# Re-cutting the side streams of a scan stage and issuing attention in written order, in a Mamba, expert, attention and FFN block on one core

## The chip, the cores and the metric

The kernel runs on one core of a Trainium2 chip. The metric is the device time in microseconds from the kernel's start to its end; times are given as the median of several runs. A profiled execution is a further run with the hardware profiler on; its span is the time from its first to its last instruction.

## The reference, cut to what matters

The input x has 4 sequences of 512 tokens and 128 channels. Four residual layers follow one another: a Mamba block with a mixture of experts behind it, an FFN, a latent attention, and the same FFN again.

```python
x = x + attn_a(layernorm(x))   # Mamba, then 8 experts, top 2
x = x + ffn(layernorm(x))      # 128 -> 384 -> 128, silu(gate) * up
x = x + attn_b(layernorm(x))   # 16 heads of 8, causal, low-rank q and k
x = x + ffn(layernorm(x))
# in attn_a, for every token t, 256 channels and 16 states:
dA = exp(delta[t] * A);  h = dA * h + (delta[t] * u[t]) * B[t];  y[t] = sum_n(h * C[t])
# then the experts:
out = out + w_e * (silu(hs @ Wg[e]) * (hs @ Wu[e])) @ Wd[e]
```

The recurrence in `h` is what makes the scans: for each of 4 sequences and 16 states one scan along 512 tokens, for 256 channels.

## The kernel before

**Tiles.** A sequence is 4 tiles of 128 tokens (NT = 4); 256 channels are 2 halves of 128 partitions (NE = 2). The program has two stages. In the first, 64 scans (4 sequences x 16 states) run one after another. In the second, attention runs over 16 groups G of 4 heads; two groups make a unit u (8 heads of one sequence), 8 units in all.

**A scan step** (`scan`, L844). For state n of sequence b: ACT makes the decay `da` (L796) two steps ahead and SP loads `cs` (L800); PE spreads a row of B over the partitions, `pb` (L806); DVE multiplies it with `du` to `bx` (L838) and scans `hst` (L858); POOL multiplies with C to `hc` (L870); PE adds `hc` over the states into `yp` with four matmuls (L816). `bx` and `pb` have one buffer each, `hst` two.

**Side streams.** All else in the first stage is written as Python generators and put beside the scans: `ahead` (the `front` of the next sequence: norm, convolution, projections, softplus), `closing` (`close`, `route`, `number`, `scatter`: gate, output projection, routing, and writing the tokens to DRAM by expert), `tokens` (`combine`, the first FFN, `project` to q and k), `tiles` (`experts`, one tile of 128 rows per step) and `rest` (`early`: statistics of the later sequences, zeros, weights). A stream's step has two halves: `begin` runs to the generator's next yield and is traced between the scan and the product `hc`; `end` runs to the yield after it and is traced behind the product `bx` of the next scan (`halves`, L569). A half that yields "sc" wants the two shared PSUM tiles of that tag; in a scan only the first stream that wants them gets its `end`, the others wait for the next scan with theirs. `hc` waits for the DVE instructions that the `begin` halves issued (L876).

**Who orders the work.** Inside `tc.manual_schedule(engines=ORDERED)` the instructions of PE, DVE, ACT and SP are issued in the order in which the code writes them. The scans and three turns after them are in such a block (L978, L1013). The second stage, from L1219 on, is not: there a planner of the language orders each engine's instructions by its own priorities.

**Experts.** Groups of sequences are [0], [1] and [2, 3], with 15, 15 and 23 tiles of rows. `experts` plans which rows belong to which expert (DVE, L272 to 299), then takes a tile per step: SP stores the tile of three steps ago, loads rows and weights (L341 to 357), PE transposes (`mpt`), forms gate and up (`mpg`, `mpu`, L370) and down (`mpd`, L382), ACT does tanh (`thm`), DVE the two products (L320, L321) at the next `begin`. `combine` gathers each token's two rows back with POOL's indirect DMAs (`yk`, L403) and adds them one turn later (L395).

**Attention.** `project` (L496) makes q and k, splits them into three bf16 parts on POOL and stores them (`q_d`, `k_d`); `fill(u)` (L1063) loads a unit's `qs` and `ks` with six DMAs on SP. `maxima(u)` (L1074) forms scores on PE and their row maxima on DVE (L1084), 22 tiles a unit, and writes the maxima into `qs` through DRAM. `exps(G)` (L1124) forms the scores again with the maxima taken off and exponentiates on ACT (`p`, L1154), ten steps a group. `weigh(G)` (L1157) multiplies by the values (f32, `po`, L1166). In the loop over G (L1230) each of ten steps takes a score, one or two maxima and a piece of the weigh of the group before; side streams get `rate` turns a step. Sequences' last FFNs (`last`) start at units 3, 5 and 7, that of sequence 3 stands alone at the end.

The roots of the layer norms are made on DVE by an integer guess and three Newton steps (`rsqrt`, L131).

Of the kernel before, what the change touches and what calls it, by code (L numbers as in the profile page):

```python
# [8 lines left out]
F32 = mybir.dt.float32  # L9
# [28 lines left out]
def block_kernel(ctx, tc, x, rms1_w, rms2_w, in_proj_w, conv_w, conv_b, x_proj_w,  # L38
# [172 lines left out]
    def number(b):  # L211

        hit = hits[b]
        both = tmp("both", [NT, NEXP], BF16)
        nc.vector.tensor_tensor(both, hit[:, :, 0], hit[:, :, 1], ALU.add)
        yield
        pr = ps.tile([P, 2, NT, NEXP], F32, tag="mm", name="prank")
        for i, m in enumerate((before, ones)):
            nc.tensor.matmul(
                pr[:, i].rearrange("p j e -> p (j e)"), m, both.rearrange("p j e -> p (j e)"),  # L220
                start=True, stop=True,
            )

        tot = tmp("ctot", [NEXP, NT])
        nc.scalar.copy(tot, pr[:, 1].rearrange("p j e -> p e j"))
        ahead = tmp("cahead", [NT, NEXP])
        nc.scalar.copy(ahead, pr[:, 0])
        yield
        inc = tmp("cinc", [NEXP, NT])
        nc.vector.tensor_tensor_scan(  # L230
            inc.rearrange("p e j -> p (e j)"), restart.rearrange("p e j -> p (e j)"),
            tot.rearrange("p e j -> p (e j)"), 0.0, ALU.mult, ALU.add,
        )
        g, at = place[b]
        free = regions[ROWS[g]] if at == 0 else taken[g]
        taken[g] = end = tmp("cend", [NEXP])
        nc.vector.tensor_tensor(end, free, inc[:, :, NT - 1], ALU.add)
        nc.vector.tensor_tensor(inc, inc, tot, ALU.subtract)
        nc.vector.tensor_tensor(
            inc, inc, free.unsqueeze(2).to_broadcast([P, NEXP, NT]), ALU.add  # L240
        )
        row = tmp("crow", [NT, NEXP])
        nc.vector.tensor_tensor(row, inc.rearrange("p e j -> p j e"), ahead, ALU.add)
        rows2 = tmp("crows", [NT, 2, NEXP])
        nc.vector.tensor_tensor(
            rows2, hit, row.unsqueeze(2).to_broadcast([P, NT, 2, NEXP]), ALU.mult
        )
        rowf = tmp("crowf", [NT, 2])
        nc.vector.tensor_reduce(rowf, rows2, AX.X, ALU.add)
        nc.vector.tensor_copy(rows[b], rowf)  # L250
        yield

    def scatter(b):
# [3 lines left out]
        for t in range(NT):  # L257
            for k in range(2):
# [6 lines left out]
                if (2 * t + k) % 3 == 2:  # L265
                    yield
                    yield
# [55 lines left out]
    def experts(g):  # L323
# [8 lines left out]
        n = NTILES[g]  # L332
        xt, xT, wgu, wd, hidden, ys, of = {}, {}, {}, {}, {}, {}, {}
        for i in range(-1, n + 3):
            if i - 2 in hidden:
# [53 lines left out]
    def combine(b):  # L389
# [3 lines left out]
        for t in range(NT + 1):  # L393
            for k, yk in enumerate(got):
                nc.vector.scalar_tensor_tensor(  # L395
                    base[b][:, t - 1, :], yk, gates[b][:, t - 1, k : k + 1],
                    base[b][:, t - 1, :], ALU.mult, ALU.add,
                )
            yield
            new = []  # L400
            for k in range(2 if t < NT else 0):
                yk = wt.tile([P, C], F32, tag="yk", name="yk", bufs=4)
# [5 lines left out]
            got = new  # L408
# [184 lines left out]
    with ExitStack() as first:  # L593
# [42 lines left out]
        for k in ("r0", "m0", "r01", "m01"):  # L636
            norms[k] = w1.tile([P, B * NT], F32, tag=k, name=k)

        def deviations(seqs):
            n = len(seqs) * NT  # L640
            cols = slice(seqs[0] * NT, seqs[0] * NT + n)
            r0, m0, r01, m01 = (norms[k][:, cols] for k in ("r0", "m0", "r01", "m01"))
            v = w1.tile([P, n], F32, tag=f"v{n}", name="v0")
            mean, var = (mv0.rearrange("p b t s -> p (b t) s")[:, cols, k] for k in range(2))
            nc.vector.tensor_scalar(v, var, EPS, None, ALU.add)
            rsqrt(v, n, w1, "ln", r0)
            less(mean, r0, n, to=m0)
            nc.vector.tensor_tensor(v, r0, r0, ALU.mult)
            nc.vector.tensor_tensor(v, v, var, ALU.mult)
            nc.vector.tensor_scalar(v, v, EPS, None, ALU.add)  # L650
            rsqrt(v, n, w1, "rms", r01)
            nc.vector.tensor_tensor(r01, r01, r0, ALU.mult)
            less(mean, r01, n, to=m01)

        def early():

            for b in range(1, B):
# [3 lines left out]
            deviations(range(1, B))  # L661
# [39 lines left out]
        def front(b):  # L701

            h0[b] = h = w2.tile([P, NT, C], F32, tag="h0", name=f"h0_{b}")
            hn = w1.tile([P, NT, C], F32, tag="hn", name="hn")
            cols = slice(b * NT, (b + 1) * NT)
            scaled(hn, xs[b], norms["r01"][:, cols], norms["m01"][:, cols])
            scaled(h, xs[b], norms["r0"][:, cols], norms["m0"][:, cols])
# [6 lines left out]
            for e in range(NE):  # L714
                yield "sc"
                pm = ps_s.tile([P, L], F32, tag="sc", name="pm")
                for k in range(KW):
                    nc.tensor.matmul(
# [3 lines left out]
                pms.append(pm)  # L722
                if e == NE - 1:
                    for i in range(NE):
                        nc.scalar.activation(xi[b][:, i, :], pms[i], AF.Silu, bias=cb[:, i, :])
                yield
            yield
# [6 lines left out]
            yield  # L734
            yield "sc"
# [7 lines left out]
            nc.scalar.copy(dt[b], pm[0:DTR, :])  # L743
            pm = ps_s.tile([P, L], F32, tag="sc", name="pbc")
# [9 lines left out]
            cr = w1.tile([2 * NS, L], F32, tag="bc_c", name="bc_c")  # L754
            nc.scalar.copy(bc[b], pm[0:96, :])
            nc.scalar.copy(cr, pm[0 : 2 * NS, :])
            c_d[b] = dram1.tile([NS, L], F32, tag="c_d", name="c_d")
            nc.sync.dma_start(c_d[b], cr[NS:, :])
            yield
            nc.vector.tensor_tensor(rest, pm[0:96, :], bc[b], ALU.subtract)  # L760
            nc.scalar.copy(mid, rest)
            yield "sc"
            nc.gpsimd.tensor_copy(bc[b][32:64, :], mid[32:64, :])
            nc.gpsimd.tensor_tensor(bc[b][64:96, :], rest[64:96, :], mid[64:96, :], ALU.subtract)
# [4 lines left out]
            du[b] = r = w2.tile([P, NE, L], F32, tag="du", name=f"du_{b}")  # L769
            for e in range(NE):  # L770
# [5 lines left out]
                nc.scalar.activation(r[:, e, :], pd, AF.Relu, bias=dtb[:, e, :])  # L776
            nc.scalar.activation(y, y, AF.Exp, scale=-1.0)
            nc.scalar.activation(dl, y, AF.Ln, bias=1.0)
            nc.scalar.activation(d, y, AF.Identity, bias=1.0)
            yield  # L780
            nc.vector.scalar_tensor_tensor(d, d, -1.0, y, ALU.add, ALU.subtract)
            yield
            yield
# [100 lines left out]
        def close(b):  # L884
# [12 lines left out]
            for t in range(NT):  # L897
                for e in range(NE):
# [3 lines left out]
                    )  # L902
            h2 = wt.tile([P, NT, C], F32, tag="h2", name="h2", bufs=1)
            nc.scalar.copy(h2, po)
            yield
            yield
            nc.gpsimd.tensor_tensor(h2, h0[b], h2, ALU.add)
            yield
# [20 lines left out]
            yield  # L929
# [6 lines left out]
            nc.scalar.copy(lg, pl)  # L936
            yield
# [40 lines left out]
        with tc.manual_schedule(engines=ORDERED):  # L978
# [5 lines left out]
            next(first)  # L984

# [18 lines left out]
            for b in range(B):  # L1004
                if b:
                    closing.add(close(b - 1), start(b - 1), scatter(b - 1))
                for n in range(NS):
                    if n == 4 and b + 1 < B:
# [11 lines left out]
    with ExitStack() as second:  # L1020
# [200 lines left out]
        while 0 not in stores:  # L1221
            turn(*streams)
        fill(0)
        fill(1)
        for _ in times(2, maxima(0)):
            turn(*streams)
        begin = {3: (0,), 5: (1,), 7: (2,)}
        rate = {0: 1.2, 1: 1.0, 2: 0.8, 3: 0.8, 4: 0.8, 5: 0.8}
        filled, credit = 2, 0.0
        for G in range(2 * UNITS + 1):  # L1230
            u = G // 2
            if G % 2 == 0:
                ends.add(*(last(b) for b in begin.get(u, ())))
                while filled < min(u + 3, UNITS) and filled // 2 in stores:
                    fill(filled)
                    filled += 1
                if u < UNITS and u % 2 == 0:
                    values(u // 2)
                while u + 1 < UNITS and filled <= u + 1:
                    turn(*streams)  # L1240
                    if filled // 2 in stores:
                        fill(filled)
                        filled += 1
                more = maxima(u + 1) if u + 1 < UNITS else iter(())
            scores = exps(G) if G < 2 * UNITS else iter(())
            weighed = weigh(G - 1) if 1 <= G else iter(())
            for step in range(10):
                credit += rate.get(u, 0.4)
                while credit >= 1.0:
                    turn(*streams)  # L1250
                    credit -= 1.0
                next(scores, None)
                next(weighed, None)
                for _ in range(1 + step % 2):
                    next(more, None)
            run(weighed)
            if G % 2 == 1:
                run(more)
        while any(stream.gens for stream in streams):
            turn(*streams)  # L1260
        run(last(B - 1))
# [56 lines left out]
```

## Time and profile before

| | us |
|---|---|
| Median of 3 runs | 958.27 |
| Lowest, highest | 956.39, 960.52 |
| Profiled execution | 962.98 |
| Its span | 960.9 |
| First scan starts, last scan starts | 49.3, 428.2 |
| First scores with exponentials | 547.1 |
| PE, DVE, ACT, POOL busy | 757.7, 565.0, 413.4, 316.0 |
| Mean granted TensorE clock | 0.852 of full |

Of the page, a group's line gives the engine, the operation, what it writes and reads, its count, its busy time in us and the mean of one in ns, and after the second bar how long the engine was idle just before these instructions and for whom it waited. Here are some of the rows that the work below uses:

```profile
L870 POOL TENSOR_TENSOR hc<-hst,cs 128x1024 f32<-128x1024 f32 x64 | 150.5, 2355 | 161.8 <-DVE mh L321 39.3
L858 DVE TENSOR_TENSOR_SCAN hst<-da,bx 128x1024 f32<-128x1024 f32 x64 | 146.3, 2286 | 6.9
L838 DVE TENSOR_TENSOR bx<-du,pb 128x1024 f32<-128x1024 f32 x64 | 78.3, 1223 | 16.4 <-PE pb L806 12.1
L1166 PE MATMUL po<-p,va 128*32 128x512 f32 (+3 forms) x512 | 73.2, 451 | 0.0
```

In lines of the timeline the first number is the start in us from the span's start, the second how long it took; what stands in brackets is the idle time before it and who ended it.

### The profile page before, as it was taken

The numbers are of one execution on the slowest core, as the hardware profiler recorded it, in microseconds if no ns is written. First come the engines' busy times: TensorE is split into PE (matmuls) and PEld (weight loads), VectorE is DVE, ScalarE is ACT, GpSimd is POOL, SyncE is SP. The second block draws the span as 40 slices with busy tenths as digits, with TensorE's granted clock in tenths as the row PEclk, the third lists the DMA queues.
The fourth block names the chain that finished last, engine by engine and source line by source line (L and its number), as shares of the span: only waits on it lengthen the run. The fifth ranks groups of instructions, "written<-read, shape, count | busy, mean of one in ns | idle before, by whom it ended". The sixth has DMA issues, their size and how long they took to land. (4 is left out here: it accounts for less than half of the span.)

```text
span 960.9 us, 11946 instructions
## 1 busy us (share of the span) xinstructions
PE 757.7 (79%) x3763; PEld 425.7 (44%) x3763; DVE 565.0 (59%) x1154; ACT 413.4 (43%) x798; POOL 316.0 (33%) x247
## 2 busy tenths in 40 slices
PE   4449777859897867887685899999569999999964
PEld 1114233227644624555553676873233435454432
DVE  3197687878777886883375543434750543666411
ACT  2635726824666432423301344443025435645641
POOL 1135474574427564563205103001404031000010
PEclk9768879959998987898857899998575959999997
DMA  3018321128424515433753546773102303120000
GB/s 101 34 33 338 126 65 56 47 81 251 149 72 139 167 56 156 123 117 121 191 128 107 173 141 221 242 197 74 33 2 80 85 19 92 37 47 3 3 12 11
DMA packets 84479, 99.16 MB, mean 103 GB/s; under 512 B 10369, under 2 KB 56457, under 8 KB 83241
## 3 DMA queue, kind: packets, MB, share of 16 engines
q1 hardware_dynamic: 78881, 87.09, 30.6%
q0 software_dynamic: 4352, 10.89, 3.7%
q8 instruction: 30, 0.49, 0.2%
q10 hardware_dynamic: 1184, 0.43, 0.2%
q14 instruction: 32, 0.26, 0.1%
HBM read 76.67 MB, written 21.63 MB: 102 GB/s over the span
## 5 line engine op out<-in xcount | busy, mean ns | idle before, releaser
L870 POOL TENSOR_TENSOR hc<-hst,cs 128x1024 f32<-128x1024 f32 x64 | 150.5, 2355 | 161.8 <-DVE mh L321 39.3
L816 PE MATMUL yp<-hc,ident 128*128 128x512 f32 x256 | 152.3, 724 | 31.3 <-POOL hc L870 29.6
L858 DVE TENSOR_TENSOR_SCAN hst<-da,bx 128x1024 f32<-128x1024 f32 x64 | 146.3, 2286 | 6.9
L1084 DVE TENSOR_REDUCE mx<-sc 128x1 f32<-128x384 f32 (+3 forms) x168 | 103.3, 635 | 69.5 <-PE sc L1092 67.8
L1154 ACT ACTIVATE p<-st 128x512 f32<-128x512 f32 x160 | 90.7, 598 | 52.6 <-PE st L1149 50.1
L816 PEld LDWEIGHTS yp<-hc,ident 128*128 128x128 f32 x256 | 53.2, 221 | 126.2 <-POOL hc L870 83.3
L1088 PE MATMUL sc<-ks,qs 72*128 72x128 bf16 (+3 forms) x256 | 78.1, 367 | 34.0 <-issue 14.2
L796 ACT ACTIVATE da<-delta,A 128x512 f32<-128x512 f32 (+1 forms) x128 | 84.5, 713 | 29.4 <-DVE hst L858 26.7
L838 DVE TENSOR_TENSOR bx<-du,pb 128x1024 f32<-128x1024 f32 x64 | 78.3, 1223 | 16.4 <-PE pb L806 12.1
L320 DVE SCALAR_TENSOR_TENSOR thm<-thm,mpg 128x512 f32<-128x512 f32 x53 | 36.1, 681 | 81.6 <-ACT thm L376 81.6
L370 PE MATMUL mpg<-xTm,wgu 128*128 128x128 f32 x424 | 67.5, 304 | 9.3 <-DVE thm L320 4.3
L1166 PE MATMUL po<-p,va 128*32 128x512 f32 (+3 forms) x512 | 73.2, 451 | 0.0
L370 PEld LDWEIGHTS mpg<-xTm,wgu 128*128 128x128 f32 x424 | 60.7, 216 | 21.4 <-issue 6.8
L1141 PE MATMUL st<-qs,ks 75*128 75x512 bf16 (+3 forms) x256 | 63.5, 317 | 1.7 <-DMA qs<-m_d 0.8
L382 PE MATMUL mpd<-wd,mh 128*128 128x128 f32 x424 | 58.8, 280 | 5.5 <-ACT xTm L363 5.3
L370 PE MATMUL mpu<-xTm,wgu 128*128 128x128 f32 x424 | 61.6, 291 | 1.1 <-DMA wgu<-in_Wu_dram 1.1
L806 PE MATMUL pb<-bc,pick 96*128 96x512 bf16 x64 | 27.5, 430 | 41.9 <-DVE bx L838 40.4
L370 PEld LDWEIGHTS mpu<-xTm,wgu 128*128 128x128 f32 x424 | 57.3, 208 | 1.6 <-issue 0.6
L382 PEld LDWEIGHTS mpd<-wd,mh 128*128 128x128 f32 x424 | 52.9, 195 | 9.4 <-ACT xTm L363 7.7
L363 ACT ACTIVATE xTm<-mpt,r2w 128x128 f32<-128x128 f32 x53 | 19.4, 367 | 87.5 <-PE mpt L361 64.6
L1092 PE MATMUL sc<-maskq,identb 128*128 128x128 bf16 (+2 forms) x176 | 51.8, 294 | 0.0
L259 POOL DMA_INDIRECT xg<-hs,rows x32 | 34.3, 1071 | 52.6 <-DVE cends L280 44.3
(244 smaller groups left out, 1111.3 us busy)
## 6 DMA issues: line engine op xcount, KB each, us to landing
cs<-c_d SPq DMA_DIRECT2D x64, 256.0 KB
wgu<-in_Wg_dram SPq DMA_DIRECT2D x53, 256.0 KB
wgu<-in_Wu_dram SPq DMA_DIRECT2D x53, 256.0 KB
wd<-in_Wd_dram SPq DMA_DIRECT2D x53, 256.0 KB
xg<-zero SPq DMA_DIRECT2D x8, 1024.0 KB
k_d<-parts POOLq DMA_DIRECT2D x12, 384.0 KB
qs<-q_d SPq DMA_DIRECT2D x24, 192.0 KB
ks<-k_d SPq DMA_DIRECT2D x24, 192.0 KB
```

Of the source, the lines that this page charges most:

```text
L370: nc.tensor.matmul(pp[:, f, :], w[:, k, f * P : (f + 1) * P], rows_in, start=True, stop=True,)
L382: nc.tensor.matmul(pd, hT[:, f, :], w[:, f, :], start=(f == 0), stop=(f == NFC - 1))
L796: nc.scalar.activation(da[:, e, e:], delta[b][:, e, e:], AF.Exp, scale=A[:, e, n : n + 1])
L816: nc.tensor.matmul(yps[b][:, e, :], ident, hc[:, e, :], start=(n == 0), stop=(n == NS - 1))
L838: nc.vector.tensor_tensor(bxs[s], du[s // NS], taps[s][1].unsqueeze(1).to_broadcast([P, NE, L]), ALU.mult)
L858: nc.vector.tensor_tensor_scan(hst.rearrange("p e l -> p (e l)"), dec.pop(s).rearrange("p e l -> p (e l)"), bxs.pop(s).rearrange("p e l -> ...
L870: done = nc.gpsimd.tensor_tensor(hc, hst, cs.unsqueeze(1).to_broadcast([P, NE, L]), ALU.mult).ins
L1084: nc.vector.tensor_reduce(*taken, AX.X, ALU.max)
L1088: nc.tensor.matmul(sc[:, c : c + w], q[0:NP9, h, t * P : w], k[0:NP9, h, 0:w], start=(h == h0), stop=False, skip_group_check=True,)
L1141: nc.tensor.matmul(pt[:, c : c + L - kt * P], k[0 : NP9 + 3, h0 + j, rows], q[0 : NP9 + 3, h0 + j, kt * P : L], start=(c == 0), stop=False ...
L1154: nc.scalar.activation(p, pt, AF.Exp, scale=scale)
L1166: nc.tensor.matmul(po[32 * j : 32 * j + 32, kt * P : L], vs[b % 2][:, kt, c : c + 32], got[j][kt], start=(kt == 0), stop=(kt == NT - 1),)
```

## The change

It has four parts.

1. **Norms of the first layer.** `deviations` makes both inverse roots (of the layer norm, and of layer norm and RMS norm together) in one `rsqrt` of double width; sequence 1's statistics move from the first scans into the prologue. `front` writes its scaled input into the tile "xn" of another pool and makes `h0` behind `sz`.
2. **Side streams in the scans.** `front` starts at a sequence's first scan instead of its fifth; the convolution's eight matmuls come in four steps instead of two; pdt, pbc and pd, and Exp, Ln and the DVE products of softplus, get steps of their own. `close` adds `h0` on DVE straight from PSUM, and has fewer empty halves; `number` ends without a yield; `scatter` issues two DMAs per step instead of three. `experts` has an empty step before its first tile step and one after it.
3. **combine** adds a gathered row two turns after its gather instead of one, with six buffers instead of four.
4. **Attention.** The whole second stage's loop stands in `tc.manual_schedule(engines=ORDERED)`. A turn's `begin` halves stand ahead of a step's score, maxima and weigh, its `end` halves behind them; the weigh comes behind the maxima. Two more turns run between the first fills and the first maxima. `rate` is 0.7 for units 0 to 4 and 0.5 beyond, instead of 1.2 falling to 0.8, then 0.4, and a step has one turn at most.

The diff, cut to its core:

```diff
 def number(b):
         nc.vector.tensor_copy(rows[b], rowf)
-        yield
 def scatter(b):
-                if (2 * t + k) % 3 == 2:
+                if k and t < NT - 1:
                     yield
                     yield
 def experts(g):
         n = NTILES[g]
+        yield
+        yield
         for i in range(-1, n + 3):
+            if i == 0:
+                yield
+                yield
 def combine(b):
-        for t in range(NT + 1):
-            for k, yk in enumerate(got):
+        for t in range(NT + 2):
+            for k, yk in enumerate(got.pop(0) if t > 1 else ()):
...
-            got = new
+            got.append(new)
 def deviations(seqs):
+            nc.vector.tensor_scalar(v[:, 0], var, EPS, None, ALU.add)
+            nc.vector.tensor_scalar(v[:, 1], var, 1.0 + EPS, EPS * EPS, ALU.mult, ALU.add)
+            rsqrt(v.rearrange("p k b t -> p (k b t)"), 2 * n * NT, w1, f"ln{n}",
+                  r.rearrange("p k b t -> p (k b t)"))
 def front(b):
                 for k in range(KW):
+                    if k % 2 == 0:
+                        yield "sc"
                     nc.tensor.matmul(
...
+                    if k % 2:
+                        yield
+            yield "sc"
             for e in range(NE):
...
+            h0[b] = w2.tile([P, NT, C], F32, tag="h0", name=f"h0_{b}")
+            scaled(h0[b], xs[b], norms["r"][:, 0, b], norms["m"][:, 0, b])
             yield "sc"
...
             nc.scalar.copy(dt[b], pm[0:DTR, :])
+            yield
+            yield "sc"
             pm = ps_s.tile([P, L], F32, tag="sc", name="pbc")
...
+            nc.vector.tensor_tensor(rest, cr, bc[b], ALU.subtract)
+            nc.scalar.copy(mid, rest)
+            yield
+            nc.gpsimd.tensor_copy(bc[b][32:64, :], mid[32:64, :])
...
             nc.scalar.activation(y, y, AF.Exp, scale=-1.0)
+            yield
+            yield
             nc.scalar.activation(dl, y, AF.Ln, bias=1.0)
             nc.scalar.activation(d, y, AF.Identity, bias=1.0)
             yield
+            if b:
+                yield
+                yield
 def close(b):
+            yield
             h2 = wt.tile([P, NT, C], F32, tag="h2", name="h2", bufs=1)
-            nc.scalar.copy(h2, po)
-            yield
-            yield
-            nc.gpsimd.tensor_tensor(h2, h0[b], h2, ALU.add)
-            yield
+            nc.vector.tensor_tensor(h2, po, h0[b], ALU.add)
 # the scans
-                    if n == 4 and b + 1 < B:
+                    if n == 0 and b + 1 < B:
                         ahead.add(front(b + 1))
 # attention
-        rate = {0: 1.2, 1: 1.0, 2: 0.8, 3: 0.8, 4: 0.8, 5: 0.8}
+        rate = {0: 0.7, 1: 0.7, 2: 0.7, 3: 0.7, 4: 0.7}
+        with tc.manual_schedule(engines=ORDERED):
...
             for step in range(10):
-                credit += rate.get(u, 0.4)
-                while credit >= 1.0:
-                    turn(*streams)
-                    credit -= 1.0
-                next(scores, None)
-                next(weighed, None)
-                for _ in range(1 + step % 2):
-                    next(more, None)
+                    credit += rate.get(u, 0.5)
+                    beside = credit >= 1.0
+                    if beside:
+                        credit -= 1.0
+                        for stream in streams:
+                            stream.begin()
+                    next(scores, None)
+                    for _ in range(1 + step % 2):
+                        next(more, None)
+                    next(weighed, None)
+                    if beside:
+                        halves(streams)
```

## The prediction

> **What bounds the kernel now.** I read the page's busy table and slices first, then the busy time and granted clock of each engine stage by stage, then the waits of VectorE (DVE) in the scans, then single stretches of the timeline. No engine bounds the whole: TensorE (PE) is busy 79% and DVE 59%.
>
> ```profile
> PE 757.7 (79%) x3763; PEld 425.7 (44%) x3763; DVE 565.0 (59%) x1154; ACT 413.4 (43%) x798; POOL 316.0 (33%) x247
> PE   4449777859897867887685899999569999999964
> ...
> PEclk9768879959998987898857899998575959999997
> ```
>
> The stages (columns: stretch, length, busy us of PE, PE's weight load, DVE, ACT, POOL, then PE's granted clock):
>
> ```profile
> 49.00:434.50 385.50, 299.81 (x1080) 160.68 (x1079) 313.28 (x455) 186.32 (x346) 212.05 (x118) 0.86 0.39 124
> 434.50:477.00 42.50, 31.77 (x186) 25.68 (x186) 12.96 (x26) 14.46 (x39) 16.24 (x14) 0.88 0.54 158
> 477.00:545.00 68.00, 48.19 (x269) 33.39 (x269) 43.99 (x133) 10.18 (x27) 17.00 (x18) 0.67 0.47 130
> 545.00:661.00 116.00, 108.60 (x817) 78.65 (x816) 40.27 (x80) 55.68 (x122) 11.34 (x13) 1.00 0.66 192
> 661.00:743.00 82.00, 59.22 (x208) 27.95 (x206) 44.39 (x143) 21.12 (x41) 26.77 (x30) 0.61 0.11 31
> 743.00:763.00 20.00, 19.20 (x132) 9.76 (x131) 7.80 (x40) 8.38 (x15) 2.35 (x2) 0.96 0.35 92
> 763.00:786.00 23.00, 21.16 (x65) 8.49 (x65) 12.62 (x31) 8.34 (x17) 4.81 (x6) 0.54 0.21 51
> 786.00:925.00 139.00, 134.84 (x910) 66.02 (x910) 67.20 (x165) 78.45 (x146) 15.78 (x19) 0.99 0.13 34
> ```
>
> From 49 to 434.5 the 64 scans run, 6.0 us each: DVE leads (313 of 385), with 72 us of gaps. From 545 on PE leads. Busy time there is no fixed amount of work[...]. Busy times granted clock gives PE's work at full clock: 109+36+18+11+133 = 308 us from 545 to 925, done in 380. So 37 us were idle (380 less 343 busy) and some 35 went to a lowered clock. The same product for 434.5 to 545 is 60 us in 110. What DVE waits for in the scans:
>
> ```profile
> DVE bx L838 <- PE pb L806: 12.1, 6, 6.0
> DVE base L395 <- DMA yk<-yg,rows_y: 9.2, 8, 2.6
> DVE thm L320 <- ACT thm L376: 8.1, 5, 3.2
> DVE sp_d L781 <- ACT sp_d L779: 7.5, 3, 4.4
> DVE best L956 <- ACT lg L936: 6.0, 2, 3.4
> DVE bc_rest L760 <- ACT bc_c L756: 5.7, 2, 2.9
> ```
>
> These six are 48.6 us: each is a side stream whose DVE part is queued one scan step after an ACT, PE or DMA part that isn't done. What order costs in the attention shows in one stretch of its timeline:
>
> ```profile
> 525.04 0.35 DVE L395 SCALAR_TENSOR_TENSOR base<-yk,gates,base 128x128 f32<-128x128 f32 x1 [6.73 <-DMA yk<-yg,rows_y]
> 525.92 0.48 PE L1088 MATMUL sc<-ks,qs 72*128 72x384 bf16 x1 [6.96 <-issue]
> ...
> 688.21 0.48 PE L1088 MATMUL sc<-ks,qs 72*128 72x384 bf16 x1 [3.40 <-DVE mv L155]
> ```
>
> DVE stands on a gathered row, the maxima behind it free no PSUM, PE stands on them.
>
> [...] the granted clock falls to 0.61 where PE idles (661 to 743), and the accumulation yp x4 takes 1.88 us in one place and 3.78 in another. [...] delta (L784) takes 2.18 us beside hc at 301.75, against 1.23 alone.
>
> **The change part by part.** I count steps by the yields in the code: a side stream gets one step (two yields) per scan, or per turn later.
>
> 1. *Prologue.* The two inverse roots for sequence 0 become one: 29 small DVE instructions to 17, at the 0.20 us from one start to the next (5.92 to 11.68): -2.4. Scaling h0 (1.63 us of ACT) leaves the place ahead of hT, whose transposes ended at 14.05 while hT began at 15.08: -1.0. Sequence 1's moments and root (about 4.6 us of DVE) go between 14 and 31, where DVE idles 16.9 us before bc_rest: nothing, and 4.6 if that cover were gone. Sum -3.5, first scan at 45.8 instead of 49.3.
>
> 2. *Scans, DVE's own work.* A scan with nothing beside it takes 3.75 (starts at 121.4 and 125.2; scan 2.29, bx 1.22, gaps), one with an expert tile's two products 4.90. Adding each step's small instructions at 0.2 us, stats at 0.84 a sequence, softplus products at 1.23, I get 333 us for the order of before and 325 for the new: the roots for sequences 2 and 3 are 14 instructions shorter and sequence 1 is gone (-4), h2 moves from ACT and POOL to DVE (3 x 0.7 = +2), and 6 of 24 pairs of halved products (1.37 each) leave the scans.
>
> 3. *Scans, gaps.* 385 less 333 leaves 52 lost in before, which the six waits explain. New: sp_d and bc_rest come two or more half-steps after their ACT parts (13.2 to 0); routing comes one scan after its logits (6 to 0); a gather gets one more turn (9.2 to 3); the convolution goes in halves of 1.7 us of PE instead of 3.4, and a tile's first transpose gets a turn more after its load, which held PE and pb at 211 for 4.0 us (bx: 12.1 to 5); thm stays (8). That is 16. Against it, four steps now put two scatters and two gathers (0.95 us each, 0.3 apart: 5 us) beside hc's 2.35 on POOL: 7.4 where DVE needs 4.5, up to +12 less what before paid for the same transfers: +8, range 0 to 12. With 4 unassigned: 325+16+8+4 = 353 against 385: -32, range -12 to -42.
>
> 4. *What is deferred.* The convolution's four steps, z, pdt, pbc and pd now claim the shared PSUM pair ("sc"), 8 a sequence instead of 4, and each holds a tile back a scan. When the last scan is issued, group 1 stands at its 4th tile step instead of the 8th, the first FFN at its first of three slices instead of done, the projection not begun. PE's deferred work: 4 tiles x 3.45 (mpg, mpu, mpd 1.06 each, mpt) + 2 slices x 2.0 + 2.5 + 0.7 = 21 us. Sequence 0 is projected 5 turns later (turn 72, not 67).
>
> 5. *From the last scan to the first scores.* Turns 64 to 79 are PE's, at 5.2 to 5.4 us by the spacing of tiles from 443 to 476 (5.5) with the maxima (1.3 a turn) filling gaps: 85. Turns 80 to 86 wait for the chain plan, row load, weight load: 20, as from rows at 511.5 to the first product at 531.6. Sum 105, against 112.6 before (434.5 to 547.1); range 90 to 120. Two turns between fill and maxima hide the 4.9 us that PE waited for ks. SP's 12 fills (472 to 480) still stand ahead of a tile's loads, as before.
>
> 6. *Attention.* The work stays near 308. The written order puts a score, maxima, a weigh (f32) and half a side step in each step, so the runs of bf16 alone that met the low clock (728 to 740, 763 to 786) vanish: lost clock 35 to 10, range 0 to 30. Idle: 6.4% as in the evenly mixed 545 to 661, 20; seven layernorms whose root (2.4) and scaling (1.65) stand in the same step as their transposes, with 2.0 us of other PE work ahead (a score 0.6, maxima 0.9, a weigh 73.2/160 = 0.46): 2 each, 14. A new stall: at a slower rate (0.7 turns a step instead of 1.2 to 0.8) sequence 2 is projected only in five turns without scores, and the maxima behind them stand on its load: root 2.4, scaling 1.65, five PE and ACT hops of 1.1, two splits on POOL at 3.0, stores 3.2 and landings, six loads: 30, less 8 of last(0) beside it: 22, range 10 to 35. Seven turns, not ten, per ten score steps cost nothing, PE being full. Sum 308+10+20+14+22 = 374, against 378 (547 to 925)[...].
>
> 7. *End.* last(3) alone, 925 to 961: 36, unchanged.
>
> 45.8+353+105+374+36 = 914 of span, against 960.9. The profiled execution took 962.98 (2.1 around its span): 916. Before's median is 0.5% under its profiled run, so 912.
>
> **The rivals.** *More*: written order at one clock brings attention near its work, 308+20+10, and POOL doesn't collide: 914-36-8 = 870, as time 868. For it: 786 to 925 ran at 0.99 with 4 us idle. Against: the load chain. *Deferral eats it*: the scans give 14 not 32 and part 5 gains nothing: 914+18+7 = 939, time 937. For it: 21 us of PE work moved from under DVE to where PE leads. *Slower*: PE in written order stands at every side turn beside the scores, as it did for DVE at 525. About 75 such turns follow; the gain ahead is 46, so it decides from 0.6 us a turn. At 1.0 us: 912+75 = 987. [...] against: the scans, also in written order, lost 52 us in 64 steps. That the order isn't as written is excluded for all but POOL: the scans' trace shows it.
>
> **Numbers.** Forecast 0.57 (890 to 932), more 0.12, deferral 0.14, slower 0.17. Range 876 to 968, which takes in part of the outer cases. About 0.5% is what a measurement can tell from no change: faster 0.78, same 0.05, slower 0.17.
>
> **What would show it.** First scan near 46; DVE's waits for sp_d, bc_rest and logits gone; last scan near 399; first scores near 504; PE's clock near 1.0 from there, but for a stall of some 20 us at the seventh group; no DVE wait on yk over 2 us. It is wrong if attention's idle time exceeds 100 us, or if scans stay at 6 us.

## The result, and the profile after

The changed kernel takes 1016.43 us (median of 4 runs, 1012.97 to 1018.09) against 957.33 us (953.47 to 960.52) beside it: ratio 1.0614, 95% interval 1.0565 to 1.0664. It is 6.1% slower; 912, with a range of 876 to 968, was forecast. The profiled execution took 1016.83 us, its span is 1015.1.

The page's busy row and slices:

```profile
PE 746.0 (73%) x3763; PEld 431.1 (42%) x3763; DVE 580.5 (57%) x1151; ACT 415.0 (41%) x794; POOL 309.9 (31%) x243
...
PE   6295697698898558755668874997754778898865
...
PEclk9697897799999759887758976998777787697887
```

PE is busy 12 us less than before in a span 54 us longer. Of the right half's 20 slices 13 had a 9 before, now 3 have. The stages (columns as before) are cut at the first scan, the start of the last scan, the first exponential and the last exponential:

```profile
43.20:394.80 351.60, 274.30 (x937) 137.77 (x936) 306.75 (x402) 175.39 (x322) 204.39 (x113) 0.87 0.39 126
394.80:534.30 139.50, 90.53 (x505) 71.79 (x506) 58.26 (x162) 29.15 (x76) 34.34 (x33) 0.76 0.46 130
534.30:978.60 444.30, 346.21 (x2215) 206.87 (x2217) 191.35 (x489) 179.68 (x350) 61.51 (x69) 0.83 0.27 75
978.60:1015.10 36.50, 16.25 (x76) 7.84 (x74) 7.96 (x29) 6.37 (x13) 2.52 (x2) 0.71 0.03 8
```

Cut by the same events (starts in us; the last column is PE's busy time in the attention):

| | first scan | last scan | first scores | last exponential | span | attention, of it PE busy |
|---|---|---|---|---|---|---|
| before | 49.3 | 428.2 | 547.1 | 925.4 | 960.9 | 378.3, 343 |
| after | 43.2 | 394.8 | 533.6 | 978.6 | 1015.1 | 445.0, 346 |
| difference | -6.1 | -33.4 | -13.5 | +53.2 | +54.2 | +66.7, +3 |

So the scans brought the 33 us that they should. Of these, 20 were gone when the first scores began, and the attention took 67 more. There PE was busy about as long as before, so nearly all of the 67 is idle time of PE: 35 us of it before, 98 after. PE's waits in the attention (from 534.3 to 978.6; us in total, times, longest):

```profile
PE sc L1104 <- DMA ks<-k_d: 24.3, 2, 12.6
PE pmx L1127 <- DVE mparts L1123: 14.0, 7, 4.4
PE sc L1104 <- DVE mx L1100: 9.9, 12, 2.3
PE sc L1104 <- issue: 7.7, 3, 6.1
PE pt L176 <- ACT axn L167: 6.2, 2, 5.8
```

The same view of before has no row for `ks` and one of 0.9 us for `mparts`. Its longest are 6.7 us for `mx` and 6.4 for `axn`. (The 6.1 beside "issue" ends at 713.36, and the profile names no cause for it. The same product stands 6.4 us for `mx` in the run with PE and DVE in written order below, so it may belong to the row of `mx`.)

One stand, that is a stretch in which an engine does nothing, from the timeline of all engines, as sequence 2 is projected in the turns without scores:

```profile
746.25 0.59 ACT L457 COPY fo<-fpd 128x512 f32<-128x512 f32 x1 [2.23 <-PE fpd L452]
...
746.54 0.27 PE L1165 MATMUL st<-maskk,identb 128*128 128x256 bf16 x1
...
746.91 1.27 POOL L458 TENSOR_TENSOR x<-base,fo 128x512 f32<-128x512 f32 x1 [5.25 <-ACT fo L457]
748.21 0.87 DVE L153 BATCH_NORM_STATS2 st<-x 128x6 f32<-128x128 f32 x4 [4.12 <-POOL x L458]
...
751.78 0.16 DVE L162 SCALAR_TENSOR_TENSOR nm<-mv,rs_r 128x4 f32<-128x4 f32 x1
...
752.03 1.65 ACT L167 ACTIVATE axn<-x,nm,rs_r 128x128 f32<-128x128 f32 x4 [4.21 <-DVE nm L162]
...
752.58 1.63 PE L176 MATMUL pt<-ident,axn 128*128 128x128 f32 x4 [5.76 <-ACT axn L167]
```

PE's next instruction in the written order is the transpose of `axn`. It waits through a copy on ACT, an addition on POOL, the statistics and the root on DVE and the scaling on ACT, one after another. Another stand is where unit 2 begins:

```profile
618.50 0.45 SPq L1086 DMA_DIRECT2D qs<-q_d  x1
...
620.22 0.22 PE L1165 MATMUL st<-maskk,identb 128*128 128x128 bf16 x1
...
628.96 0.29 SPq L1086 DMA_DIRECT2D ks<-k_d  x1
...
632.17 0.59 PE L1104 MATMUL sc<-ks,qs 72*128 72x128 bf16 x4 [11.73 <-DMA ks<-k_d]
```

In the code, the loads of units 2 and 3 stand directly ahead of the maxima of unit 2. SP's twelve DMAs go out from 618.5 to 629, and PE stands from 620.4 to 632.2 on their first product. DVE, whose order is written too, does nothing in these 11.7 us.

### The profile page after: what moved, and what is told of

The parts are those of the page before. It is cut to its first block, busy times and chain, and to the rows that moved or that the text cites. A ratio compares the mean times of both kernels' runs of the same rounds, so it can differ in the third digit from the quotient of the medians.

```text
span 1015.1 us, 11919 instructions
## 1 busy us (share of the span) xinstructions
PE 746.0 (73%) x3763; PEld 431.1 (42%) x3763; DVE 580.5 (57%) x1151; ACT 415.0 (41%) x794; POOL 309.9 (31%) x243
## 4 chain that ended last, share of the span: by engine, by line
PE 39%; DVE 27%; issue 8%; DMA 8%; POOL 8%; ACT 7%; SPq 2%; POOLq 0%; DVEq 0%; ACTq 0%
DVE hst L874 8%; PE po L1182 4%; PE mpg L374 4%; DVE bx L854 3%; PE mpu L374 3%; PE yp L832 3%; PE st L1157 3%; PE sc L1104 3%; POOL hc L886 3%; PE mpd L386 3%; PE pg L443 2%; DVE mx L1100 2%; PE fpd L452 2%; DMA ks<-k_d 2%; POOL xg L258 1%
## 5 line engine op out<-in xcount | busy, mean ns | idle before, releaser
L1170 ACT ACTIVATE p<-st 128x512 f32<-128x512 f32 x160 | 94.0, 598 | 70.3 <-PE st L1165 59.7
L1104 PE MATMUL sc<-ks,qs 72*128 72x128 bf16 (+3 forms) x256 | 71.2, 345 | 49.0 <-DMA ks<-k_d 24.3
L1157 PE MATMUL st<-qs,ks 75*128 75x512 bf16 (+3 forms) x256 | 69.8, 339 | 8.1 <-ACT p L1170 4.8
L374 PE MATMUL mpu<-xTm,wgu 128*128 128x128 f32 x424 | 65.0, 304 | 0.4 <-DMA wgu<-in_Wu_dram 0.4
L386 PE MATMUL mpd<-wd,mh 128*128 128x128 f32 x424 | 61.0, 291 | 3.0 <-issue 1.8
L374 PEld LDWEIGHTS mpu<-xTm,wgu 128*128 128x128 f32 x424 | 60.4, 220 | 0.6 <-DVE mx L1100 0.5
L386 PEld LDWEIGHTS mpd<-wd,mh 128*128 128x128 f32 x424 | 56.7, 208 | 3.6 <-issue 2.0
L1182 PE MATMUL po<-p,va 128*32 128x128 f32 (+3 forms) x512 | 54.7, 506 | 0.0
L407 POOL DMA_INDIRECT yk<-yg,rows_y x32 | 31.2, 976 | 69.9 <-DMA yg<-ym 57.2
L1108 PE MATMUL sc<-maskq,identb 128*128 128x128 bf16 (+2 forms) x176 | 48.8, 277 | 0.0
```

Source lines behind the costliest of these rows:

```text
L374: nc.tensor.matmul(pp[:, f, :], w[:, k, f * P : (f + 1) * P], rows_in, start=True, stop=True,)
L386: nc.tensor.matmul(pd, hT[:, f, :], w[:, f, :], start=(f == 0), stop=(f == NFC - 1))
L1104: nc.tensor.matmul(sc[:, c : c + w], q[0:NP9, h, t * P : w], k[0:NP9, h, 0:w], start=(h == h0), stop=False, skip_group_check=True,)
L1157: nc.tensor.matmul(pt[:, c : c + L - kt * P], k[0 : NP9 + 3, h0 + j, rows], q[0 : NP9 + 3, h0 + j, kt * P : L], start=(c == 0), stop=False ...
L1170: nc.scalar.activation(p, pt, AF.Exp, scale=scale)
L1182: nc.tensor.matmul(po[32 * j : 32 * j + 32, kt * P : L], vs[b % 2][:, kt, c : c + 32], got[j][kt], start=(kt == 0), stop=(kt == NT - 1),)
```

## The experiments

**1 to 4: which part.** The first takes all of after up to the attention loop, and the loop of before; the second is the reverse. The third is after without the written order in the second stage:

```diff
-        with tc.manual_schedule(engines=ORDERED):
+        if True:
             while 0 not in stores:
```

The fourth issues loads early, in written order:

```diff
-        rate = {0: 0.7, 1: 0.7, 2: 0.7, 3: 0.7, 4: 0.7}
+        rate = {0: 0.8, 1: 0.8, 2: 0.8, 3: 0.7, 4: 0.7}
...
                 for step in range(10):
+                    while filled < min(u + 3, UNITS) and filled // 2 in stores:
+                        fill(filled)
+                        filled += 1
```

New scans alone: 

> First stage and side streams as after, attention loop as before (planner orders it, old rates). Theory A (the written order of the attention costs the time): only the earlier scans remain, first scores 27 to 33 us earlier than before, attention near 378 us: 920 to 930 us. Rival B (work deferred from the scans costs the time wherever it lands): the 21 us of PE work and the five later turns show here too: 950 to 980 us.

New attention loop alone: 

> First stage and side streams as before, attention loop as after (written order, slower rates, halves). Theory A: scans as before and the whole loss of the second stage, 20 + 67 us: 1030 to 1050 us. Rival B: the old streams leave nothing deferred, so 955 to 985 us.

The planner in place of the written order: 

> After, with one line changed: the second stage is not in the block of written order, so the planner orders it; rates, halves and the two added turns stay. Theory A: most of the 87 us comes back: 925 to 945 us. Rival C (the slower rates and the place of the halves cost the time, whoever orders): 990 to 1015 us.

Early loads: 

> After, with written order, but a unit's loads are issued at the first step at which the stores are there, not only where a unit begins, and units 0 to 2 get 0.8 turns a step instead of 0.7 so that no turns stand without scores ahead of unit 3. Theory A1 (loads queued right ahead of their maxima are the main part): PE's two waits for ks, 24.3 us, go and the clock recovers with them: 975 to 990 us. Rival A2 (many small waits in written order are the main part): 24 us less at most, 990 to 1005 us, attention idle still over 70 us.

| | median us | ratio to before, 95% | last scan | first scores | attention |
|---|---|---|---|---|---|
| new scans alone | 948.52 | 0.9898 (0.9834 to 0.9962) | 396.8 | 522.9 | 390.0 |
| new loop alone | 1020.92 | 1.0691 (1.0620 to 1.0761) | 424.3 | 561.7 | 415.1 |
| planner | 943.97 | 0.9881 (0.9822 to 0.9941) | 395.1 | 526.0 | 380.6 |
| early loads | 1008.15 | 1.0533 (1.0459 to 1.0606) | 395.6 | 535.8 | 434.0 |

(Each run has runs of before beside it; their medians lie between 953.5 and 957.3, and the ratios are to these.) The planner kernel settles the largest point: one line taken back turns 6.1% slower into 1.2% faster. Rates, halves and the two added turns cost nothing by themselves, when the planner orders the stage. The new loop costs as much on the old scans, so what the scans defer isn't needed for it either; its time is 9 us under theory A's range. The new scans alone miss theory A's range and fall just under B's. A last scan 31 us earlier brings 13 us of span (960.9 to 947.8): 7 are given back between scans and scores and 12 in the attention. "Deferral eats it" had the 7, but sought its other 18 in the scans, which gave their gain in full. The 12 in the attention need not be deferral's: the planner's run below has the same scans and 380.6 us. Early loads miss both ranges upward. Of the 24.3 us for `ks` 16.8 stay, and `mx` rises to 14.7, `xt` to 12.6.

The window of the planner's attention (columns as before):

```profile
526.70:906.60 379.90, 346.29 (x2152) 192.67 (x2152) 180.01 (x471) 174.41 (x345) 61.21 (x69) 0.93 0.30 84
```

PE is busy 346.29 us here and 346.21 in after, so the profile has all of the 64 us between them as idle time. (Equal busy time isn't equal work, as the runs with PE's written order below show.) The longest waits of its PE there:

```profile
PE po L1182 <- issue: 4.7, 1, 4.7
PE sc L1104 <- DVE mx L1100: 4.0, 18, 0.4
PE st L1157 <- DMA qs<-m_d: 3.5, 1, 3.5
PE mpg L374 <- DMA wgu<-in_Wg_dram: 2.6, 4, 1.0
PE pmx L1127 <- DVE mparts L1123: 2.5, 1, 2.5
```

`ks` is gone, though most of unit 2's and 3's loads go out as the unit begins here too (581.1, and 591.8 to 601.6): the planner's order has scores, weighs and expert products of PE in the meantime.

**5 to 8, 11, 12: whose order.** Each is after with the written order left on some of the four engines in the second stage; an engine that is freed is ordered by the planner. For example:

```diff
-        with tc.manual_schedule(engines=ORDERED):
+        with tc.manual_schedule(engines={ENG.PE}):
```

PE freed: 

> After, but in the second stage only DVE, ACT and SP keep the written order; the planner orders PE. Theory A-PE (PE in written order stands on late operands and holds everything behind them): nearly all of the 72 us that the planner gave back comes back here: 945 to 960 us. Rival A-DVE (DVE's written order delays the maxima and the roots, PE only waits for it): 1000 to 1015 us.

DVE freed: 

> After, but in the second stage the planner orders DVE; PE, ACT and SP keep the written order. Theory A-PE: 1000 to 1016 us, since PE still stands at the same places. Rival A-DVE: 945 to 965 us.

SP freed: 

> After, but in the second stage the planner orders SP, which may issue a unit's loads and a tile's weights earlier; PE, DVE and ACT keep the written order. Theory A-PE: 985 to 1010 us, at most the 24 us that PE waits for ks and the 15 for xt come back. Rival A-SP (late loads are the root of it): 950 to 975 us.

PE alone written: 

> After, but in the second stage only PE keeps the written order; the planner orders DVE, ACT and SP. Theory A-PE: 990 to 1016 us. Rivals A-DVE and A-SP: 945 to 965 us, since what PE waits for comes earlier.

DVE alone written: 

> After, but in the second stage only DVE keeps the written order; the planner orders PE, ACT and SP. PE alone in written order cost 18 us over the planner's 944, and DVE, ACT and SP together 28. Theory K (the cost comes from queues in written order together): DVE alone costs 0 to 12 us: 944 to 956 us. Rival V (DVE's order is most of those 28): 962 to 975 us.

PE and DVE written: 

> After, but in the second stage only PE and DVE keep the written order; the planner orders ACT and SP. Alone, PE's order cost 18 us over the planner's 944, and DVE's 16. Theory S (their costs add): 975 to 981 us. Theory K (each stands on what the other has queued behind its own stand, so that together they cost more than the sum): 985 to 997 us. Rival M (the two stand at the same places, so that the second costs little more): 960 to 970 us.

| written order on | median us | ratio to before, 95% | points over the planner's 0.9881 |
|---|---|---|---|
| none | 943.97 | 0.9881 (0.9822 to 0.9941) | 0 |
| DVE | 959.81 | 1.0041 (1.0015 to 1.0067) | 1.6 |
| PE | 962.52 | 1.0055 (1.0027 to 1.0083) | 1.7 |
| DVE, ACT, SP | 971.59 | 1.0169 (1.0132 to 1.0205) | 2.9 |
| PE, ACT, SP | 982.00 | 1.0283 (1.0223 to 1.0342) | 4.0 |
| PE, DVE, ACT | 994.93 | 1.0410 (1.0374 to 1.0447) | 5.3 |
| PE, DVE | 999.97 | 1.0495 (1.0438 to 1.0552) | 6.1 |
| all four (after) | 1016.43 | 1.0614 (1.0565 to 1.0664) | 7.3 |

Only SP freed came out in the range of theory A-PE; freeing PE brings back 45 us and freeing DVE 34, both between the ranges. That PE's order alone holds everything falls: with PE alone in written order the kernel takes 962.5, not 990 or more, which is in the rivals' range. Nor does DVE's order or SP's account for it alone. PE and DVE together cost 6.1 points, the two by themselves 3.3 in sum; 1000 us is 3 above the range of the theory that they cost more together, and 19 above the range in which they add. DVE alone missed both ranges, since it costs 16 us and not 0 to 12. No cost of ACT's order is seen beside PE's and DVE's (5.3 against 6.1). If it costs nothing elsewhere either, SP's adds 1.3 points to DVE's, 2.3 to PE's and 2.0 to both; SP's order by itself was not run. The waits of PE in the attention, with PE alone in written order:

```profile
PE sc L1104 <- DMA ks<-k_d: 13.3, 1, 13.3
...
PE sc L1104 <- DVE mx L1100: 8.6, 13, 1.8
...
PE pmx L1127 <- DVE mparts L1123: 4.3, 4, 1.3
```

and with PE and DVE:

```profile
PE sc L1104 <- DMA ks<-k_d: 22.9, 2, 14.0
PE sc L1104 <- DVE mx L1100: 17.0, 15, 6.4
PE pmx L1127 <- DVE mparts L1123: 13.5, 7, 4.4
```

The instructions of PE come in the same order in both. With DVE in written order too, its maxima and their splitting come later, and PE's waits for them grow from 12.9 to 30.5 us. The loads don't make the difference: the other stand of 8.9 us at `ks` is there with PE alone as well, as 8.5 us put down to `yg`. With only DVE written, PE waits 1.1 us for `ks` and 5.1 for `mx`: it does other things. The windows of the two attentions:

```profile
524.60:924.60 400.00, 327.92 (x2217) 196.12 (x2220) 185.90 (x476) 179.53 (x350) 61.21 (x69) 0.86 0.30 84
531.00:959.70 428.70, 340.99 (x2217) 204.22 (x2220) 192.02 (x489) 180.95 (x350) 61.74 (x69) 0.84 0.28 78
```

So 16 of the 29 us between them are idle time of PE, and 13 are longer busy time of the same instructions, at a lower granted clock (0.84 against 0.86).

**9: distance in the written order.** In `ffn` and in `project` a turn more, in `maxima` two pieces more, loads in each step as in the fourth experiment, and higher rates (beyond unit 4 0.6 instead of 0.5):

```diff
 def ffn(src, dst):
         yield from layernorm(xn, src)
+        yield
+        yield
...
 def maxima(u):
+            yield
+            yield
             pm = ps.tile([3 * NU, L], BF16, tag="mm", name="pmx")
...
-        rate = {0: 0.7, 1: 0.7, 2: 0.7, 3: 0.7, 4: 0.7}
+        rate = {0: 0.9, 1: 0.9, 2: 0.9, 3: 0.7, 4: 0.7}
```

> After, with written order on all four engines, but with distance put between a result and its use: a unit's loads are issued as soon as its stores are there; side streams run 0.9, 0.7 and 0.6 turns a step instead of 0.7 and 0.5, so that stores come earlier; the maxima's transposes stand two pieces behind their splitting on DVE, and a layer norm's transposes one turn behind its scaling. Theory N (PE stands on operands written too close to their use): the waits for ks, mparts, axn and xn, 49 us in after, nearly vanish and little comes in their place: 960 to 980 us. Rival K (four queues in written order hold one another up; a stand that is mended reappears elsewhere): at least half of it comes back under other names, 985 to 1010 us.

It took 1024.51 us, ratio 1.0708 (1.0650 to 1.0767): slower than either theory said. The first scores came at 546.2, 12.6 us later than in after (the first FFN and the projection have a turn more each). The attention took 436.5 us, 8.5 less, with 111 us idle, 13 more. Its longest waits of PE there:

```profile
PE st L1163 <- DMA qs<-m_d: 25.9, 4, 10.5
PE sc L1108 <- DVE mx L1104: 18.0, 16, 3.7
PE st L1163 <- ACT p L1176: 9.8, 3, 5.0
PE mpt L365 <- DMA xt<-xg: 9.4, 2, 4.8
PE st L1163 <- DMA qs<-q_d: 9.1, 1, 9.1
```

The rows for `ks`, `mparts`, `axn` and `xn`, 49 us in after, are gone from the top. In their place the scores stand on the maxima's way through DRAM (25.9), which starts two pieces later, and on `qs` (9.1). That agrees with rival K's mechanism, though the total doesn't fall at all. It is not proof of it, since rates and loads were changed together with the distances.

**10: fewer claims.** The planner's kernel, with the convolution in two steps and pbc in pdt's:

```diff
-                    if k % 2 == 0:
+                    if k == 0:
                         yield "sc"
...
-                    if k % 2:
+                    if k == KW - 1:
                         yield
...
             nc.scalar.copy(dt[b], pm[0:DTR, :])
-            yield
-            yield "sc"
```

> As the kernel whose second stage the planner orders (944 us), but the streams claim the shared PSUM pair five times a front instead of eight: the convolution comes in two steps, and pbc in pdt's. Theory D (deferral: each claim holds a tile back and its 3.45 us of PE work lands where PE leads): three tile steps come back into the scans, which get some 3 us longer, and the second stage gets 8 to 12 us shorter: 935 to 941 us. Rival (the convolution's longer piece of PE work holds up pb and the scan again, as it did before): 944 to 950 us.

It took 936.92 us, ratio 0.9764 (0.9714 to 0.9813), 7 us under the planner's kernel, in theory D's range, and the fastest here. The last scan starts at 398.7, 3.6 later; from there to the first scores it takes 117.9 us instead of 130.9; the attention takes 385.0 instead of 380.6. Only the middle one stands clear of the spread: in the ten other profiled runs with after's first stage the last scan starts at 394.8 to 398.4 and the stretch takes 126.1 to 140.2 us. So deferral is shown to cost, and the place is the stretch between scans and scores. (That the planner found a luckier order for a slightly different program was not ruled out.)

## Why the prediction was wrong

The prediction cut the scans at the last product `hc`. It starts at 398.6 after, 434.5 before.

1. *Prologue: -3.5.* Measured -6.1 (first scan at 43.2). Right in kind; the other kernels with this prologue began at 43.4 to 45.4.
2. *DVE's own work: 333 to 325.* DVE is busy 310.3 us (43.2 to 398.6) against 313.1 before (49.3 to 434.5), 3 us less. But in after 10.7 us of this, and 1.6 in before, are what a few instructions took beyond the shortest of their kind (see 3). Without these it is 12 us less, so the 8 were right in kind.
3. *Scans: 353.* Measured 355.4 (43.2 to 398.6), right in sum. The waits of DVE there:

```profile
DVE fwg L693 <- DMA raw<-in_w_gateT_dram: 10.3, 1, 10.3
DVE base L399 <- DMA yk<-yg,rows_y: 6.3, 4, 2.9
DVE thm L319 <- ACT thm L380: 5.5, 4, 2.7
DVE bx L854 <- PE pb L822: 3.4, 3, 2.1
```

   `sp_d`, `bc_rest` and the logits are gone, 19.2 us, as said; `bx` fell from 12.1 to 3.4 (said: 5). `yk` fell to 6.3, not 3. POOL's clash, put at 8, shows as waits of only 1.3 (`hst` for `hc`), but it is there. The three scans with two gathers and two scatters beside `hc` took 6.8, 7.4 and 7.4 us, as the working had it (7.4 where 4.5 are needed), 8 more in sum. Of this 3.3 are waits for `yk`; most of the rest hides in DVE's busy time:

```profile
362.07 2.35 POOL L886 TENSOR_TENSOR hc<-hst,cs 128x1024 f32<-128x1024 f32 x1
362.39 2.58 DVE L399 SCALAR_TENSOR_TENSOR base<-yk,gates,base 128x128 f32<-128x128 f32 x2 [1.31 <-DMA yk<-yg,rows_y]
```

   The first of these two `base` took 2.19 us beside `hc`, the second 0.35 behind it; three such cases add 5.5 us. Two `sp_d` took 3.68 and 3.69 us beside `hc` instead of 1.20, another 5.0 that the working hadn't. It hadn't, either, 10.3 us for a weight (2.7 before): `early` reaches its scaling sooner, and one scan took 14.2 us. The eight stores of zeros (1 MB each) go out from 60.84 on, this load at 87.69; that it waits for them is argued, not tried.
4. *Deferral.* Right: the fourth tile of group 1 was transposed at 394.9, as the last scan began.
5. *Scans to scores: 105.* It took 135.0 (398.6 to 533.6). Two terms failed. "Turns 64 to 79 are PE's, at 5.2 to 5.4 us" took the spacing of tiles for that of turns: the first fill comes at 467.2, 68.6 us after the last `hc`, for turns 64 to 72, some 7.6 us each. And "Two turns between fill and maxima hide the 4.9 us" had it backwards: the tile in those turns loads behind the twelve fills. The working saw the fills "ahead of a tile's loads", but put nothing on them. The queue of SP:

```profile
467.15 0.46 SPq L1086 DMA_DIRECT2D qs<-q_d  x1
...
476.27 0.29 SPq L1086 DMA_DIRECT2D ks<-k_d  x1
...
479.28 0.36 SPq L353 DMA_DIRECT2D xt<-xg  x1
```

   PE's transpose of this tile stood 13.3 us, till 486. Against before this stretch grew by 20 us from the last scan's start: in these single profiled runs some 8 are the written order's (the planner takes 130.9 of after's 138.8), 12 the deferral's (experiment 10 is back at 117.9, before has 118.9).
6. *Attention: 374.* It took 445.0, and this is **the step that failed**. "Idle: 6.4% as in the evenly mixed 545 to 661, 20" carried over the idle share of a stretch that the planner had ordered, and "lost clock 35 to 10" promised a gain from the mix that no trace had shown. The lines that were to show what order costs, at 525 and 688, also come from the planner's stage. In the sum's own terms the 445 us are 287 of work (346 busy at 0.83), 59 of lost clock and 98 idle, where 308, 10 and 56 (20, 14 and 22) were said. The terms that were listed fit: PE idled 24 us from 746.8 to 788.1, at the seventh group (22 said), and layernorms' transposes stood 10.5 in all (14 said, 5.8 of them within that stretch). What was not listed are the other uses right behind their making: unit 2's loads 11.7, the splitting of the maxima 14.0 in seven stands, maxima 9.9 (6.7 before), `mT` 4.7. The planner's run has only 2.5 us for the splitting, 4.0 for the maxima and none for `ks`. "Idle time exceeds 100 us", put down as a sign of being wrong, was missed by 2 us.
7. *End: 36.* Measured 36.5.

The rival "Slower" named the side and the place but not the mechanism. PE standing at side turns is there, yet PE's written order alone costs 18 us; it takes DVE's order beside it for 56. A stand of one engine may delay what the other's next instruction needs. In the two stands shown above, nothing that is written later ran on the engine that stood: PE was busy 0.00 us of the 5.76, and in the 11.7 us of PE and DVE together PE 0.04 (the end of a product begun before) and DVE 0.00. Under the planner other instructions stand next to each other. That the two orders cost more together than in sum is shown (6.1 points against 3.3); that this is the way in which they do is argued from the rows of waits. Which of the stands start such a round is not settled, nor why spacing four of them (experiment 9) brought the attention only 8.5 us. Only this written order and experiment 9's were tried; how much a better one would cost is open.

The clock was read wrongly too. "Busy times granted clock gives PE's work at full clock" would make 287 us of work in after and 322 in the planner's kernel, for nearly the same instructions (2215 and 2152) and the same 346 us busy. Where PE's order is the same, the product nearly is too: 282 us with PE alone written, 286 with PE and DVE, 287 in after, while busy time grows from 328 to 341 and 346. So it compares only runs with one order of PE; why another order changes it is open. The "runs of bf16 alone that met the low clock" weren't alone either: from 763 to 786 f32 products (`pq`, `pu`) of 2.07 us a pair stand among them. Around the stand of unit 2 in after the granted clock is 0.79 before it (606 to 620.4), 0.58 in it and 0.51 just behind it:

```profile
620.40:632.10 11.70, 0.04 (x1) 0.00 (x0) 0.00 (x0) 0.89 (x2) 0.00 (x0) 0.58 0.77 155
632.10:636.00 3.90, 3.83 (x18) 1.68 (x19) 0.00 (x0) 0.37 (x1) 0.00 (x0) 0.51 0.86 169
636.00:650.00 14.00, 13.70 (x126) 10.71 (x125) 6.57 (x11) 5.36 (x12) 0.00 (x0) 1.00 0.65 185
```

After 11.7 us of standing PE works 3.9 us at 0.51, then at 1.00. A low clock doesn't always end so soon. In before, behind a stand of 1.8 us at 763.99:

```profile
766.00:788.00 22.00, 21.15 (x63) 8.13 (x63) 9.80 (x20) 7.14 (x15) 4.81 (x6) 0.50 0.12 33
```

PE was busy 96% of these 22 us, its longest wait was about 0.2 us, and the clock stayed at 0.50. What keeps it low there is not shown.

## What to carry to other kernels

A written order on several engines can cost more than the sum of what it costs on each (here 6.1 points against 3.3 for PE and DVE). Before writing it for a loop whose side work has long chains, list every place in which a result is used in the step in which it is made, loads included, and price each at the whole chain; idle time measured under a planner is no estimate for it. To see whose order costs, free the engines singly and in pairs, since the costs need not add. Work that leaves a stage because of a claim on a shared buffer has to be paid in the next stage: here the stretch behind the scans took 131 us under the planner, and 118 with three claims a front fewer. And look for a clash of two engines in the length of instructions too, since it need not show as a wait (here 0.35 us became up to 2.19).

## What was not expected of the hardware

- PE's busy time did not follow the mean granted clock alone: with the same order of PE it grew from 328 us at a mean granted clock of 0.86 to 346 at 0.83, and the planner's order took 346 at 0.93. One pair of score products (`st`, two of 75x384) takes 0.39 us at 704.07 (granted clock 1.00 from 703.5 to 705) and 0.63 at 714.60 (0.50 from 714 to 715.5), so a factor of 1.6; ends of matmuls are modelled in the profile, which limits what this says.
- An addition on DVE of 0.35 us took 2.14 to 2.19 us the three times that it ran beside `hc` on POOL, and the profile counts all of it as busy. `sp_d` took 3.68 and 3.69 us beside it instead of 1.20 (at 186.42 and 272.90). `delta`, which the prediction had seen in before, is a further case: 2.18 us beside `hc`, 1.20 to 1.23 otherwise.
